# Delta * u of a unit in three transfers, and B and C laid out in DRAM in the order of the partitions

## The chip, the cores and the metric

The kernel runs on one core of one Trainium2 chip. The metric is the time of one execution on the device, in microseconds (us), less being better. The profile is one such execution; the median is taken over several. The engines are named as in the profile: PE (matrix engine; PEld is its weight load), DVE (vector engine), ACT (scalar engine), POOL (GpSimd) and SP (the sync engine, which only issues DMAs here). "SPq" is SP's queue of instructions.

## The reference

The reference is a network of four layers on an input of 4 images of 64 x 64 pixels with 96 channels. Layers 0 and 1 are the ones that matter here. Each normalises its input, projects it to E = 192 channels, applies a depthwise 3 x 3 convolution and SiLU, and then runs a selective scan in four directions (K = 4: rows, columns, and both reversed) along the L = 4096 pixels, with N = 16 states for each channel:

```
delta = softplus(dt_w @ dts + bias)          # [B, K, E, L]
dA = exp(delta[..., None] * A)               # A: [K, E, N]
h  = dA * h + delta[..., None] * b[:, :, None, :] * u[..., None]
y  = einsum('bken,bkn->bke', h, c)
```

`u` is the convolved input in the order of the direction; `b` and `c` (16 states each) and `dts` are projections of it that differ from pixel to pixel. The four directions' `y` are put back into the order of the pixels and added, a layer norm, a gate and an output projection follow, and the result is added to the input. Layers 2 and 3 are attention without softmax and a quantised MLP; the change doesn't touch them.

## The kernel before

**Phases.** `run` goes through four phases: two layers, each on two pairs of images. A phase has two stages. `prepare` convolves both images and computes, for every direction and every chunk of TC = 512 pixels, Delta (softplus), Delta * u, B and C, and stores them in DRAM; the `finish` of the phase before runs interleaved with it. `scan_phase` then does the recurrence. After the four phases `token_layers` does layers 2 and 3.

**What is in DRAM.** For each of the NC = 8 chunks there is `ph.delta[c]` (three bf16 parts of Delta), `ph.du[c]` with shape [2, G, E + PITCH, TC] in f32 (two equal copies of Delta * u; G = 8 is directions x images) and `ph.bc[c]` with shape [G, 2 * NS, TC] (B and C, 32 rows for each of the eight g). `steps` writes them: `bc` by a DMA on ACT's queue (line 301), the two copies of `du` by one DMA each on ACT's and SP's queue (line 319), Delta on ACT's queue (line 323).

**Units of the scan.** A scan's 128 partitions are 4 quarters x 8 g x 4 states; so partition 32 a + 4 g + s holds state 4 a + s of g. A unit is one chunk of 512 pixels and EB = 12 channels. A chunk has 16 units, a phase 128, and the four phases 512. For a unit the kernel

- loads Delta (`load_delta`, line 376, tile `dlt`, three buffers) and Delta * u (`load`, `load_quarters`, line 396) into `u.h`, [128, 12, 512] in f32, of which there are four buffers. The DMA reads each row of Delta * u four times, once for every state of a quarter. Each of the three groups of quarters (1 and 2 together, 0, 3) is loaded in two halves of 6 channels, so there are six transfers: two of 64 partitions and four of 32;
- multiplies `h` by B on POOL (`times_b`, line 406), three channels at a time, four instructions a unit;
- replicates Delta over the partitions on PE (line 412), takes exp(A * Delta) on ACT (line 416) and scans on DVE (line 423), one instruction for each of the 12 channels;
- contracts over the states with C on PE (line 441), evicts on ACT (line 453) and stores with four DMAs on SP's queue (`store`, line 461).

B and C are loaded once for a chunk (`load_b`, `load_c`; `load_states`, line 344) by four DMAs each, one for every quarter:

```
for a in range(4):
    self.nc.sync.dma_start(t[32 * a : 32 * a + 32], of[:, 4 * a : 4 * a + 4])
```

**The order.** `scan_phase` writes the order out by hand; no scheduler changes it. POOL's product runs half a unit (B_LEAD = 6 channels) ahead of the scan. At the last channel of a unit SP's queue gets, in this order, the four stores of the unit before, perhaps a load of B (after unit 8 of a chunk) or of C (after unit 15, two chunks ahead), then Delta and Delta * u of the unit three ahead. There are 7 loads of B and 6 of C inside each phase; one of B and two of C stand at its start.

**Semaphores of the DMAs.** The DMAs of all queues are dealt eight semaphores in turn; a DMA that gets one waits until the DMA that had it before, eight places earlier, has landed. Inside the scan all DMAs are SP's.

Of the kernel before, what the change touches and what calls it, by code (L numbers as in the profile page):

```python
# [9 lines left out]
F32 = mybir.dt.float32  # L10
# [14 lines left out]
NS = 16  # L25
R = 6
K = 4
G = 2 * K
PAD = HW + 2
TC = 512  # L30
NC = L // TC
ROWS = TC // HW
EB = 12
# [40 lines left out]
def rows(t):  # L74

    if len(t.shape) == 2:
        return t.rearrange("p (r w) -> p r w", w=HW)
    return t.rearrange("p h (r w) -> p h r w", w=HW)
# [49 lines left out]
class Scans:  # L128
# [19 lines left out]
    def prepare(self, ph):  # L148

        nc, cst, a, pre = self.nc, self.cst, self.a, ph.pre  # L150
        ph.gs = self.keep.tile([C, 2, 2], F32, name="gs", bufs=3)
        ph.delta = [
            self.dram.tile([NP16, G, E, TC], BF16, name="delta", bufs=2 * NC) for _ in range(NC)
        ]


        ph.du = [
            self.dram.tile([2, G, E + PITCH, TC], F32, name="du", bufs=2 * NC) for _ in range(NC)
        ]
        ph.bc = [self.dram.tile([G, 2 * NS, TC], F32, name="bc", bufs=2 * NC) for _ in range(NC)]  # L160
        ph.ud = self.dram.tile([C, 2, HW, 2, 64], F32, name="ud")
        ph.y = self.dram.tile([64, G, 2, 2, NEB, 16 * EB], F32, name="y")
        x = ph.x_in[ph.pair]

        with self.tc.tile_pool(name="prep", bufs=1) as wp, self.tc.tile_pool(
            name="steps", bufs=2
        ) as sp:

            def load(name, shape, at=0):
                t = wp.tile([at + shape[0]] + shape[1:], F32, name=name)  # L170
                nc.sync.dma_start(t[at:], a[pre + name])
                return t

            xp = load("x_proj", [C, 2, 2, XD2])
            dt_w = load("dt_w", [XD2 - 2 * NS, 2, E], at=2 * NS)
            conv_b = load("conv_b", [C, 2])
            ds = load("Ds", [C, 2, K])
            dsum = wp.tile([C, 2], F32, name="dsum")
            nc.vector.tensor_reduce(dsum, ds, mybir.AxisListType.X, ALU.add)
            yield  # L180


            st = wp.tile([C, 2, 8, 6], F32, name="st")
            with self.tc.tile_pool(name="stats", bufs=2) as rp:
                for hl in range(8):
                    raw = rp.tile([C, 8, 2, 64], F32, name="raw")
                    nc.sync.dma_start(raw, x[:, hl * 8 : hl * 8 + 8])
                    for i in range(2):
                        nc.vector.bn_stats(st[:, i, hl], raw[:, :, i])
                    yield  # L190
            for i in range(2):
                mv = wp.tile([C, 2], F32, name="mv")
                nc.vector.bn_aggr(mv, st[:, i].rearrange("p c s -> p (c s)"))
                ps = self.bank()
                nc.tensor.matmul(ps[:C, :1], cst.group, mv[:, 0:1], start=True, stop=True)
                gs = ph.gs[:, i]
                nc.vector.tensor_copy(gs[:, 0:1], ps[:C, :1])
                d = wp.tile([C, 1], F32, name="d")
                nc.vector.tensor_tensor(d, mv[:, 0:1], gs[:, 0:1], ALU.subtract)
                nc.vector.scalar_tensor_tensor(d, d, d, mv[:, 1:2], ALU.mult, ALU.add)  # L200
                ps = self.bank()
                nc.tensor.matmul(ps[:C, :1], cst.group, d, start=True, stop=True)
                ln = wp.tile([C, 2], F32, name="ln")
                neg_rsqrt(nc, cst, ps[:C, :1], ln[:, 0:1], gs[:, 1:2], ln[:, 1:2])
                nc.vector.tensor_scalar_mul(gs[:, 1:2], gs[:, 1:2], -1.0)
                yield
            in_w = wp.tile([C, E], F32, name="in_w")
            nc.sync.dma_start(in_w, a[pre + "in_proj_w"][:, :E])
            taps = wp.tile([C, 9, E], F32, name="taps")
            nc.sync.dma_start(taps, a[pre + "conv_w"].unsqueeze(0).broadcast_to([C, 9, E]))  # L210

            nc.vector.tensor_tensor(
                taps, taps, in_w.unsqueeze(1).broadcast_to([C, 9, E]), ALU.mult
            )

            xc = [wp.tile([C, 2, L], F32, name="xc", bufs=2) for _ in range(2)]
            yield from self.convolve(ph, 0, x, xc[0], taps, conv_b, dsum)
            ph.beside = 0.5
            other = self.convolve(ph, 1, x, xc[1], taps, conv_b, dsum)
            for i in range(2):  # L220
                for c in range(NC):
                    for k in range(2):
                        yield from self.steps(ph, sp, xc[i], xp, dt_w, i, k, c)
                        for _ in range(2):
                            next(other, None)
                            yield
                for _ in other:
                    yield
                ph.beside = 1.7
# [52 lines left out]
    def steps(self, ph, sp, xc, xp, dt_w, i, k, c):  # L282


        nc, cst = self.nc, self.cst
        u = scan_view(xc, k, c)
        ps = self.bank()
        for h in range(2):
            nc.tensor.matmul(rows(ps[:XD2]), xp[:, k, h], u[:, h], start=h == 0, stop=h == 1)  # L289
        xd = sp.tile([XD2, TC], F32, name="xd")  # L290

        nc.scalar.activation(xd[:XD], ps[:XD], AF.Identity, bias=cst.one_row[:XD])  # L292
        nc.scalar.activation(
            xd[64:], view(ps[64:XD2], TC - 1, (-1, TC)), AF.Identity, bias=cst.one_row[64:]
        )
        yield
        both = []
        for back in range(2):
            at = 64 * back
            g, cc = 2 * (k + 2 * back) + i, NC - 1 - c if back else c  # L300
            nc.scalar.dma_start(ph.bc[cc][g], xd[at : at + 2 * NS])
            both.append((g, cc, scan_view(xc, k + 2 * back, cc), self.p_d.tile([C, 2, TC], F32, name="d")))
        for m in range(2):
            for back, (_, _, _, ps) in enumerate(both):
                part = slice(64 * back + 2 * NS, 64 * back + XD)
                nc.tensor.matmul(  # L306
                    ps[:, m], dt_w[part, k, m * C : (m + 1) * C], xd[part], start=True, stop=True
                )
        yield
        for g, cc, u, ps in both:  # L310
            delta = sp.tile([C, 2, TC], F32, name="dl")
            parts = sp.tile([C, NP16, 2, TC], BF16, name="parts")
            du = sp.tile([C, 2, TC], F32, name="du_sb")
            nc.scalar.activation(delta, ps, AF.Softplus)  # L314
            nc.scalar.copy(parts[:, 0], delta)
            nc.vector.tensor_tensor(rows(du), rows(delta), u, ALU.mult)  # L316
            nc.vector.tensor_tensor(delta, delta, parts[:, 0], ALU.subtract)  # L317
            for copy, queue in enumerate((nc.scalar, nc.sync)):
                queue.dma_start(ph.du[cc][copy, g, :E].rearrange("(h e) t -> e h t", h=2), du)
            nc.gpsimd.tensor_copy(parts[:, 1], delta)  # L320
            nc.vector.tensor_tensor(parts[:, 2], delta, parts[:, 1], ALU.subtract)  # L321
            for h in range(2):
                nc.scalar.dma_start(
                    ph.delta[cc][:, g, h * C : (h + 1) * C].rearrange("n q t -> q n t"),
                    parts[:, :, h],
                )
            yield
# [10 lines left out]
        ph.carry = self.keep.tile([128, E], F32, name="carry")  # L338
        ph.b, ph.c, ph.cw = {}, {}, {}

    def load_states(self, t, of):

        for a in range(4):
            self.nc.sync.dma_start(t[32 * a : 32 * a + 32], of[:, 4 * a : 4 * a + 4])

    def load_b(self, ph, c):
        ph.b[c] = self.units.tile([128, TC], F32, name="b")
        self.load_states(ph.b[c], ph.bc[c][:, :NS])

    def load_c(self, ph, c):  # L350
        ph.c[c] = self.units.tile([128, TC], F32, name="c")
        self.load_states(ph.c[c], ph.bc[c][:, NS:])

    def weights(self, ph, c, op):

# [25 lines left out]
    def load(self, u):  # L381

        nc, ph = self.nc, u.ph
        u.h = self.units.tile([128, EB, TC], F32, name="h", bufs=4)
        self.load_delta(u)
        n = EB // 2
        for first, quarters in ((1, 2), (0, 1), (3, 1)):
            for e in range(0, EB, n):
                self.load_quarters(u, e, n, first, quarters)

    def load_quarters(self, u, e, n, first, quarters):

# [591 lines left out]
```

## Time and profile before

| | |
|---|---|
| median of 3 runs | 12483.71 us (12462.94 to 12492.15) |
| the profiled execution | 12443.48 us, its span 12441.7 us |
| mean granted PE clock | 0.665 |
| busy share of the span: PE, DVE, ACT, POOL | 81%, 75%, 58%, 59% |
| DMA | 2491.45 MB, 882704 packets, mean 200 GB/s |
| issues of h<-du | 1024 of 768.0 KB and 2048 of 384.0 KB |
| issues of b<-bc and of c<-bc | 128 each, of 64.0 KB |
| scans of the four phases, first to last | 1909.5, 1910.9, 1912.1 and 1928.4 us |

The span is cut by the profile into engines' busy shares, but the stages have different limits: the four scan phases take 7661 us of the 12442 together, and what a change inside them is worth is read from them. A DMA that the profile shows on SPq is only its issue; the data moves later, and the DMA share and GB/s tell of that. The DMA share is the mean over 16 DMA engines. In the chain of waits, "DMA h<-du" is the time in which the chain stood on a transfer of Delta * u.

### The profile page before, as it was taken

How to read it: one execution, taken by the hardware profiler on the slowest of the kernel's cores; microseconds unless marked ns; L12 is line 12 of the kernel's file. 1: busy time of each engine (PE TensorE's matmuls, PEld its weight loads, DVE VectorE, ACT ScalarE, POOL GpSimd, SP SyncE). 2: the span in 40 equal slices, each digit the busy share in tenths (PEclk: the TensorE clock that was granted, in tenths of full speed). 3: DMA queues.
4: the chain of work that ended last, by engine and by line, in shares of the span. 5: the costliest groups of instructions: out<-in, count | busy, mean ns of one | idle time of the engine just before them, and what ended most of it. 6: DMA issues, size and time to landing. Idle time of an engine off the chain costs nothing.

```text
span 12441.7 us, 340858 instructions
## 1 busy us (share of the span) xinstructions
PE 10107.0 (81%) x147008; PEld 4972.1 (40%) x147008; DVE 9376.9 (75%) x9235; ACT 7185.6 (58%) x11815; POOL 7386.0 (59%) x2316
## 2 busy tenths in 40 slices
PE   7758888879878888879878888888878888887777
PEld 2224444433334444433334444443334444444333
DVE  2479999963569999982469999992459999993567
ACT  2456666644456666653456666663446666662556
POOL 0159999950149998960139899880129989990000
PEclk8665565669675555659775656558776655557787
DMA  3567676754667676764566777664567666663110
GB/s 92 172 227 247 244 248 247 248 168 140 213 205 246 245 247 244 250 200 128 176 215 244 246 247 249 243 226 125 174 202 249 244 243 245 245 244 122 30 21 11
DMA packets 882704, 2491.45 MB, mean 200 GB/s; under 512 B 279058, under 2 KB 561840, under 8 KB 737456
## 3 DMA queue, kind: packets, MB, share of 16 engines
q1 hardware_dynamic: 552496, 2163.38, 50.6%
q10 hardware_dynamic: 328704, 306.26, 8.5%
q8 instruction: 1158, 18.97, 0.7%
q14 instruction: 346, 2.83, 0.1%
HBM read 1955.42 MB, written 513.80 MB: 198 GB/s over the span
## 4 chain that ended last, share of the span: by engine, by line
DMA 53%; PE 20%; SPq 8%; DVE 7%; ACT 4%; issue 4%; POOL 3%; ACTq 1%; POOLq 0%; DVEq 0%
DMA h<-du 47%; PE c L260 8%; SPq L396 7%; POOL h L406 3%; PE f L591 2%; DVE h L423 2%; PE d L306 2%; DMA yk<-y 1%; PE c L289 1%; PE f L600 1%; POOL parts L320 1%; PE f L682 1%; DMA du<-du_sb 1%; PE y L441 1%; DVE parts L321 1%
## 5 line engine op out<-in xcount | busy, mean ns | idle before, releaser
L406 POOL TENSOR_TENSOR h<-h,b 128x1536 f32<-128x1536 f32 x2048 | 7016.6, 3456 | 780.6 <-DMA h<-du 369.0
L423 DVE TENSOR_TENSOR_SCAN h<-a,carry,h 128x512 f32<-128x512 f32 x5376 | 6356.7, 1259 | 391.8 <-POOL h L406 360.9
L416 ACT ACTIVATE a<-a,a_col 128x512 f32<-128x512 f32 x6144 | 4030.3, 662 | 1966.6 <-PE a L412 1814.4
L441 PEld LDWEIGHTS y<-h,cw 128*32 128x32 f32 x131072 | 2886.3, 145 | 3597.6 <-issue 1606.1
L441 PE MATMUL y<-h,cw 128*32 128x48 f32 x131072 | 3702.1, 269 | 438.0 <-ACT a L416 216.9
L412 PE MATMUL a<-dlt,rep 24*128 24x512 bf16 x6144 | 3319.4, 551 | 884.8 <-DVE h L423 782.1
L320 POOL CAST parts<-dl 96x1024 bf16<-96x1024 f32 x256 | 341.3, 1348 | 3092.1 <-DVE dl L317 2785.6
L316 DVE TENSOR_TENSOR du_sb<-dl,xc 96x1024 f32<-96x1024 f32 x256 | 397.3, 1577 | 1296.2 <-ACT dl L314 1234.8
L453 ACT COPY d<-y 128x384 f32<-128x384 f32 x2048 | 979.6, 478 | 485.7 <-PE y L441 432.7
L260 PE MATMUL c<-xn,taps 96*96 96x512 f32 x2304 | 1034.1, 609 | 73.5 <-DVE xn L245 71.0
L423 DVE TENSOR_TENSOR_SCAN h<-a,h 128x512 f32<-128x512 f32 x768 | 869.6, 1201 | 189.0 <-ACT a L416 110.6
L412 PEld LDWEIGHTS <-rep 24*128 24x128 bf16 x6144 | 471.9, 101 | 903.6 <-issue 451.0
L306 PE MATMUL d<-xd,dt_w 7*96 7x512 f32 x1024 | 520.8, 859 | 254.9 <-ACT xd L292 225.6
L260 PEld LDWEIGHTS c<-xn,taps 96*96 96x96 f32 x2304 | 382.6, 167 | 707.5 <-issue 628.7
L823 POOL MEMSET tn<- 1x4096 f32 x8 | 27.8, 3506 | 865.0 <-PE pa L843 514.7
L267 ACT ACTIVATE xc<-c,conv_b 96x512 f32<-96x512 f32 x128 | 87.3, 682 | 718.1 <-PE c L260 633.2
L591 PE MATMUL f<-yk,perm 128*128 128x384 f32 x1024 | 415.9, 546 | 99.6 <-DMA yk<-y 88.8
L314 ACT ACTIVATE dl<-d 96x1024 f32<-96x1024 f32 x256 | 252.0, 1017 | 400.9 <-DMA delta<-parts 234.5
L321 DVE TENSOR_TENSOR parts<-dl,parts 96x1024 bf16<-96x1024 f32 x256 | 366.9, 1455 | 153.2 <-POOL parts L320 153.1
L289 PE MATMUL c<-xc,x_proj 96*103 96x512 f32 x512 | 420.2, 958 | 4.2 <-ACT xc L267 4.2
L306 PEld LDWEIGHTS d<-xd,dt_w 7*96 7x96 f32 x1024 | 151.7, 212 | 542.4 <-ACT xd L292 295.8
L360 ACT ACTIVATE cw<-c,gmask 128x256 f32<-128x256 f32 x512 | 287.9, 573 | 126.2 <-DMA h<-du 65.9
(114 smaller groups left out, 5650.6 us busy)
## 6 DMA issues: line engine op xcount, KB each, us to landing
h<-du SPq DMA_DIRECT2D x1024, 768.0 KB
h<-du SPq DMA_DIRECT2D x2048, 384.0 KB
delta<-parts ACTq DMA_DIRECT2D x512, 288.0 KB
dlt<-delta SPq DMA_DIRECT2D x512, 288.0 KB
du<-du_sb SPq DMA_DIRECT2D x256, 384.0 KB
du<-du_sb ACTq DMA_DIRECT2D x256, 384.0 KB
y<-d SPq DMA_DIRECT2D x2048, 48.0 KB
yk<-y SPq DMA_DIRECT2D x256, 384.0 KB
```

What stands on the lines that cost most here:

```text
L260: nc.tensor.matmul(rows(ps[:C]), taps[:, tap, h * C : (h + 1) * C], xn[:, ROWS * c + dy : ROWS * (c + 1) + dy, dx : dx + HW], start=tap == ...
L289: nc.tensor.matmul(rows(ps[:XD2]), xp[:, k, h], u[:, h], start=h == 0, stop=h == 1)
L306: nc.tensor.matmul(ps[:, m], dt_w[part, k, m * C : (m + 1) * C], xd[part], start=True, stop=True)
L321: nc.vector.tensor_tensor(parts[:, 2], delta, parts[:, 1], ALU.subtract)
L396: self.nc.sync.dma_start(u.h[32 * first : 32 * (first + quarters), e : e + n].rearrange("p e t -> p (e t)"), source.rearrange("a g e t -> ...
L406: self.nc.gpsimd.tensor_tensor(h, h, b, ALU.mult)
L412: self.nc.tensor.matmul(u.a[n], rep, u.dl[:, n], start=True, stop=True)
L416: self.nc.scalar.activation(u.a[n], u.a[n], AF.Exp, scale=u.ph.a_col[:, at : at + 1])
L423: self.nc.vector.tensor_tensor_scan(u.h[:, n], u.a.pop(n), u.h[:, n], 0.0 if u.c == 0 else u.ph.carry[:, at : at + 1], ALU.mult, ALU.add,)
L441: self.nc.tensor.matmul(view(u.y[32 * j : 32 * j + 32], l2 * EB, (8 * EB, 4), (1, EB)), u.ph.cw[u.c][:, l1, 8 * j + l2], view(u.h, 64 * l1 ...
L453: self.nc.scalar.copy(u.d[:, :, :, l1], u.y[:, : 32 * EB].rearrange("p (t h x) -> p t h x", t=4, h=2))
L591: nc.tensor.matmul(ps[:, : 4 * C].rearrange("p (w v e) -> p w v e", w=4, v=nv), cst.perm[:, k], view(t, off, (sw if k < 2 else -sw, 4), (1 ...
```

## The change

Three things are changed. Delta * u of a unit is loaded by one transfer for each of the three groups of quarters, with all 12 channels in it: three transfers, one of 64 partitions and two of 32, with rows of 12 x 512 f32 (24 KB) where they were 12 KB. In DRAM `ph.bc[c]` is laid out as [8, G, 4, TC]: first four blocks of 4 states of B, then four of C, and inside each block the eight g; this is the order of the scan's partitions. So B, or C, of a chunk is one contiguous piece of 128 rows, and `load_states` reads it by one DMA in place of four. The DMA of `steps` that stores B and C of one g writes 8 blocks of 4 rows, where it wrote 32 rows in a row. The number of stores, the order of the instructions on the other engines, and the buffers stay as they are.

```diff
-        ph.bc = [self.dram.tile([G, 2 * NS, TC], F32, name="bc", bufs=2 * NC) for _ in range(NC)]
+        ph.bc = [self.dram.tile([NS // 2, G, 4, TC], F32, name="bc", bufs=2 * NC) for _ in range(NC)]
...
-            nc.scalar.dma_start(ph.bc[cc][g], xd[at : at + 2 * NS])
+            nc.scalar.dma_start(ph.bc[cc][:, g], xd[at : at + 2 * NS])
...
-    def load_states(self, t, of):
+    def load_states(self, ph, c, first, name):
 
-        for a in range(4):
-            self.nc.sync.dma_start(t[32 * a : 32 * a + 32], of[:, 4 * a : 4 * a + 4])
+        t = self.units.tile([128, TC], F32, name=name)
+        of = ph.bc[c][first : first + NS // 4]
+        self.nc.sync.dma_start(t, of.rearrange("a g s t -> (a g s) t"))
+        return t
 
     def load_b(self, ph, c):
-        ph.b[c] = self.units.tile([128, TC], F32, name="b")
-        self.load_states(ph.b[c], ph.bc[c][:, :NS])
+        ph.b[c] = self.load_states(ph, c, 0, "b")
 
     def load_c(self, ph, c):
-        ph.c[c] = self.units.tile([128, TC], F32, name="c")
-        self.load_states(ph.c[c], ph.bc[c][:, NS:])
+        ph.c[c] = self.load_states(ph, c, NS // 4, "c")
...
-        n = EB // 2
         for first, quarters in ((1, 2), (0, 1), (3, 1)):
-            for e in range(0, EB, n):
-                self.load_quarters(u, e, n, first, quarters)
+            self.load_quarters(u, 0, EB, first, quarters)
```

In the built program each unit then has eight DMAs on SP's queue (four stores, Delta, three of h) where it had eleven.

## The prediction

> **What bounds the kernel now.** I first read the chain of waits on the page, then the costliest groups, then the timeline of the SP queue and of POOL in one stretch of the first scan phase, and last the windows over the same stretch.
>
> The chain says that the end is set in the four scan phases, by one transfer:
>
> ```profile
> DMA 53%; PE 20%; SPq 8%; DVE 7%; ACT 4%; issue 4%; POOL 3%; ACTq 1%; POOLq 0%; DVEq 0%
> DMA h<-du 47%; PE c L260 8%; SPq L396 7%; POOL h L406 3%; PE f L591 2%; DVE h L423 2%; PE d L306 2%; DMA yk<-y 1%; PE c L289 1%; PE f L600 1%; POOL parts L320 1%; PE f L682 1%; DMA du<-du_sb 1%; PE y L441 1%; DVE parts L321 1%
> ```
>
> The groups give the floors of the two busiest engines:
>
> ```profile
> L406 POOL TENSOR_TENSOR h<-h,b 128x1536 f32<-128x1536 f32 x2048 | 7016.6, 3456 | 780.6 <-DMA h<-du 369.0
> L423 DVE TENSOR_TENSOR_SCAN h<-a,carry,h 128x512 f32<-128x512 f32 x5376 | 6356.7, 1259 | 391.8 <-POOL h L406 360.9
> ...
> L423 DVE TENSOR_TENSOR_SCAN h<-a,h 128x512 f32<-128x512 f32 x768 | 869.6, 1201 | 189.0 <-ACT a L416 110.6
> ```
>
> There are 4 x 128 = 512 units. POOL needs 7016.6/512 = 13.7 us for one, DVE (6356.7 + 869.6)/512 = 14.1 us. From the scans' start times, the units of a whole chunk (16) take 241.6 us on average (chunks 1 to 6), 15.1 each: an ordinary unit 14.1 to 15, and two in each chunk 17 to 19. So something above DVE sets the pace. The windows (columns: stretch, its length, busy time of PE, PEld, DVE, ACT, POOL, PE clock, DMA share, GB/s) show what:
>
> ```profile
> 1469.00:1473.50 4.50, 3.55 (x87) 1.83 (x81) 3.59 (x5) 3.15 (x6) 4.50 (x2) 0.50 0.91 289
> 1474.50:1482.00 7.50, 6.80 (x135) 3.28 (x134) 7.50 (x8) 5.78 (x11) 7.50 (x3) 0.50 0.56 229
> ...
> 1496.00:1501.00 5.00, 3.92 (x70) 1.69 (x71) 4.78 (x5) 3.76 (x6) 3.94 (x2) 0.50 0.29 98
> 1503.00:1507.00 4.00, 3.94 (x80) 1.83 (x73) 4.00 (x4) 2.96 (x7) 4.00 (x2) 0.50 0.97 345
> ```
>
> The DMA share swings between nearly 1 (16 engines at work, the 64-partition transfers of h) and about half (the 32-partition ones run on 8 engines). I take it from the packet records (start, duration, size) that 8 engines are never idle in an ordinary unit: the median of the time with fewer than 8 packets in flight is 0.0 us a unit. **The eight DMA engines that every transfer uses are the bound**, just above DVE. The third row is the exception, 98 GB/s. The SP queue shows what happens there:
>
> ```profile
> 1488.47 4.19 SPq L461 DMA_DIRECT2D y<-d  x4
> 1493.93 6.19 SPq L344 DMA_DIRECT2D c<-bc  x4
> 1500.23 0.65 SPq L376 DMA_DIRECT2D dlt<-delta  x1
> 1501.06 4.06 SPq L396 DMA_DIRECT2D h<-du  x6
> ```
>
> Every DMA waits for the one eight places before it: eight semaphores are dealt out in turn. A load of h has six transfers, so the four of C wait for its third to sixth: the last C is issued (1499.48) only when the whole load has landed, and Delta and h of the next unit stand behind it. The engines run dry, and POOL pays one load later (last bracket: idle before, releaser):
>
> ```profile
> 1497.86 13.71 POOL L406 TENSOR_TENSOR h<-h,b 128x1536 f32<-128x1536 f32 x4 [1.06 <-DMA c<-bc]
> 1516.06 13.66 POOL L406 TENSOR_TENSOR h<-h,b 128x1536 f32<-128x1536 f32 x4 [4.48 <-DMA h<-du]
> ```
>
> From the packet records a chunk loses 5.7 us of eight-engine time on average (chunks 1 to 6 of all phases), nearly all of it in the units after its two loads, B and C: 2.85 us for each. Without that, and without the B and C packets (1.34 us a load, below), a unit costs these engines (241.6 - 5.7 - 2.7)/16 = 14.6 us.
>
> [...] In the trace, too, one of the eight landings of a transfer often comes 1 to 2 us after the other seven. [...]
>
> **The change part by part.**
>
> (a) *One transfer for B or C.* With 3 transfers of h a unit issues 4 stores of y, 1 Delta, 3 h: eight, as many as the semaphores, so each waits for its namesake of the unit before. The B or C shifts this by one: it waits for the last Delta, Delta for the first h, the first h for the second, the second h for the third. Estimate of the room: POOL starts on a unit when its h has landed, the scan follows 3.5 us later, so the previous unit's stores can be issued about 14.6 - 3.5 = 11.1 us before that landing; four stores (0.6 each) and Delta (0.7) later the first h is reached some 7.8 us ahead, or at worst when the second h lands, 3.7 us ahead (786 KB at 213 GB/s, which the records show with eight packets in flight). The engines never run dry. There are 7 such B and 6 such C loads a phase: 52 x 2.85 = **148 us** gained. Bounds 0 (a wait remains) and 166 (by DVE's excess, 3.2 us each).
>
> (b) *Engines for B and C.* Now 4 x 32 packets of 2 KB on 8 engines, 16 each; [...] At 84 ns (records) 0.67 us less, x52 = **35 us**. Bounds 0 and 50.
>
> (c) *24 KB rows.* A unit's h packets on a busy engine fall from 24 of 12 KB to 12 of 24 KB. Fastest packets: 2 KB 84 ns, 12 KB 460, 16 KB 611, so about 37 ns per KB and some 10 ns fixed. 12 x 10 ns = 0.12 us a unit, for some 125 units of 4 phases **60 us**. No packet of this path above 12 KB is there before, so both bounds are open: 32 ns fixed (slope 8 to 12 KB) would give 190, but DVE's floor caps it; and 24 KB packets may be slower, below.
>
> (d) *Halves given up.* POOL's first piece of a unit needed only the first halves, so five of the six transfers; now it needs all three. That is one 393 KB transfer, 1.85 us at 213 GB/s. The loop that could bind is: unit u ends, stores and issue 3.3 us, h 14.6, landing 1, POOL 3.5, scans 14.1, unit u+3 ends: about 37.1 us, now 38.9, against 3 x 14.5 = 43.5. It has 4.6 us to spare, so the delay is paid once a phase: **-7 us**. Bounds 0 and, if it shows after every dry spell, 100.
>
> (e) *SP.* Three issues less in each unit and three for each B or C, of about 0.65 us. Nothing: the queue waits for landings. If DMA were faster, these would be its margin.
>
> (f) *Stores of B and C* (256, ACT queue) now write 8 blocks of 4 rows, so 8 engines instead of 16: 4 packets each instead of 2, 0.17 us, x256 = 44 us of engine time in the preparation, where the DMA share is 0.35 to 0.57 and the chain names PE, DVE and POOL. Nothing; bounds 0 and 44 lost.
>
> Sum: 148 + 35 + 60 - 7 = 236 us. Against the profiled execution, 12443.5 us: 12207. The median of the runs shown is 40 us above it; on that, 12248, rounded to 12250.
>
> After it a unit costs DMA about 14.5 us, DVE 14.1: DMA still binds, and what is late next is POOL's wait for h.
>
> **Rivals.**
> *The dry spell stays* (10%): SP reaches the first h later than worked out, and the single B or C still empties the engines. Only b, c and d: 88 us, 12396. For it: SP is always late today. Against: it is late because of six transfers' semaphores.
> *DVE becomes the bound* (9%): a 24 KB packet saves 40 ns or more. A chunk then takes 16 x 14.1 = 225.6 us, 16 less, for 7 chunks of 4 phases 448 us: 12036. Against: the sizes' slope shows 10 to 32 ns.
> *24 KB packets are slow* (slower; 9%). Place: the eight busy engines, 12 packets a unit. Without c the gain is 176 us over 500 units, 0.35 us each, 29 ns a packet: from 3% over two 12 KB packets the gain is gone. At 8%, 74 ns, 0.88 us a unit, it is 12484 - 176 + 444 = 12752; at 5%, 46 ns, 12584. For it: instruction fetches of 16 KB take 945 ns or more in the records, far above the slope. Against: 16 KB rows of the output take 611 ns, on the slope.
> *Both cancel* (6%): 3%, about 12484.
>
> **How the numbers follow.** The sum as worked out has 66%, its own range 12160 to 12330 from the bounds of a to d. A measurement of this kernel can tell about 0.2%, 25 us, from no change. Faster 66 + 10 + 9 = 85%, same 6%, slower 9%. The range takes in the main case, the first rival and part of the second: 12080 to 12440.
>
> **What would show it.** Right: in the windows no stretch near 100 GB/s beside c<-bc or b<-bc; no unit of 17 us and more; POOL's wait for h<-du well under 369 us; h<-du still first in the chain; 24 KB packets at about 910 ns. Wrong: ordinary units above 14.6 us, packets above 950 ns, or dry spells still there.

## The result, and the profile after

The changed kernel is slower. Its median is 13285.36 us (13206.6 to 13376.66, 4 runs) against 12480.49 us (4 runs) for the kernel before: a ratio of 1.065, with a 95% interval of 1.058 to 1.072. The forecast was 12250, with a range that ended at 12440.

The profiled execution took 13300.82 us, its span 13299.0, which is 857 us more than before. All of it lies in the scan phases: first to last scan they take 2155.0, 2079.8, 2143.2 and 2148.3 us, 8526 together, against 7661. The preparation didn't change. Delta * u is now 512 issues of 1536 KB and 1024 of 768 KB. In what follows the three transfers of a unit are H1 (partitions 32 to 95), H2 (0 to 31) and H3 (96 to 127). By the records of the landings all 512 H1 ran on 16 engines and all 1024 H2 and H3 on 8. That it is the same eight each time is taken from the DMA share, which is only 0.48 between 1522 and 1525 us (windows below), with an H1, an H2 and an H3 under way at once. "The eight" are these engines.

The chain of waits of the kernel after, by engine and by line:

```profile
DMA 68%; PE 18%; DVE 4%; ACT 4%; issue 3%; SPq 1%; POOL 1%; ACTq 1%; DVEq 0%; POOLq 0%
DMA h<-du 63%; PE c L260 7%; PE f L589 2%; PE d L306 2%; DMA yk<-y 1%; PE c L289 1%; DMA delta<-parts 1%; PE f L598 1%; POOL parts L320 1%; PE f L680 1%; PE f L669 1%; DVE parts L321 1%; DVE dl L317 1%; DMA du<-du_sb 1%; PE f L655 1%
```

h<-du has grown from 47% to 63% of a longer span. SPq, which held 8% before, is down to 1%: the issuing of DMAs has left the chain, and their landing fills it. The costliest groups of POOL and DVE in the kernel after:

```profile
L404 POOL TENSOR_TENSOR h<-h,b 128x1536 f32<-128x1536 f32 x2048 | 7006.0, 3452 | 1638.9 <-DMA h<-du 857.8
L421 DVE TENSOR_TENSOR_SCAN h<-a,carry,h 128x512 f32<-128x512 f32 x5376 | 6364.2, 1259 | 1128.4 <-POOL h L404 1097.4
```

The work is the same to 0.2% (7006.0 and 6364.2 us of busy time). The idle time ahead of it is not: POOL's has doubled, DVE's has nearly trebled. The wait for h<-du, which was to fall well under 369 us, is 857.8.

The chain in one stretch of the first phase (start, length, what) shows the form of the new wait. Each piece runs from the issue of an H3 to its landing, and the next H3 is issued 0.02 us later:

```profile
1491.75 17.75 DMA h<-du
1509.50 0.02 issue
1509.52 17.86 DMA h<-du
1527.38 0.02 issue
1527.39 16.32 DMA h<-du
1543.72 0.02 issue
1543.74 16.82 DMA h<-du
```

An H3 is on its way for the whole of a unit. The timeline of SP's queue in the same stretch (a group of three starts with the issue of H1 and ends with that of H3):

```profile
1510.28 3.03 SPq L459 DMA_DIRECT2D y<-d  x4
1513.40 0.69 SPq L376 DMA_DIRECT2D dlt<-delta  x1
1516.10 11.96 SPq L394 DMA_DIRECT2D h<-du  x3
1528.16 3.27 SPq L459 DMA_DIRECT2D y<-d  x4
```

The stores and Delta are out early; the three transfers of h are not. In this group H1 is issued at 1516.10, H2 at 1521.54 and H3 at 1527.39 us, and by the records of the landings their namesakes of the unit before land at 1516.01, 1521.52 and 1527.38. So each of the three stands at the head of the queue until its namesake has landed, and with it all that is behind. In 444 of the 512 units the namesake is the DMA eight places before; a load of B or C, or the start of a phase, shifts the others. Over the whole kernel 93% of the H1, 97% of the H2 and 88% of the H3 are issued within 0.15 us of the landing of the DMA eight places before. The list of SP's waits for h, for the kernel after and then for the kernel before (us in total, times, longest):

```profile
SPq L394 <- DMA h<-du: 5192.1, 1395, 8.2
SPq L376 <- DMA h<-du: 117.8, 58, 4.0
```

```profile
SPq L396 <- DMA h<-du: 2039.9, 1326, 4.0
SPq L461 <- DMA h<-du: 633.0, 657, 2.8
SPq L376 <- DMA h<-du: 571.3, 450, 2.8
SPq L344 <- DMA h<-du: 277.5, 227, 2.9
```

That is 5310 us now against 3522 before. SP waited for h all along; it waits longer now.

The windows over the stretch (columns: stretch, its length, busy time of PE, PEld, DVE, ACT, POOL, PE clock, DMA share, GB/s) show what the engines of the DMA do meanwhile:

```profile
1519.00:1522.00 3.00, 2.81 (x67) 1.61 (x67) 3.00 (x4) 1.99 (x4) 3.00 (x2) 0.50 0.93 377
1522.00:1525.00 3.00, 2.80 (x55) 1.25 (x59) 3.00 (x4) 2.10 (x4) 1.34 (x1) 0.50 0.48 156
...
1527.40:1530.00 2.60, 2.28 (x65) 1.65 (x66) 0.00 (x0) 1.31 (x4) 2.46 (x1) 0.50 0.45 115
```

By the packet records 3.7 packets are in flight on average between 1527 and 1528 us, 2.2 in the next microsecond, 10 in the one after: seven of the eight have run out of work, one has not, and H3 lands only when that one is through. A unit of a chunk took 15.1 us on average before and takes 268.2/16 = 16.8 now.

The records of the landings tell how late that one is. Of the eight landings of a 32-partition transfer the last came 0.73 us after the seventh before the change (median) and comes **8.9 us** after it now. This distance is called the lag below. The spread, from the first of the eight landings to the last, was 2.9 us and is 10.2 us.

### The profile page after: what moved, and what is told of

Same layout as the page of the kernel before. It is cut to its first block, busy times and chain, and to the rows that moved or that the text cites. A ratio compares the mean times of both kernels' runs of the same rounds, so it can differ in the third digit from the quotient of the medians.

```text
span 13299.0 us, 337534 instructions
## 1 busy us (share of the span) xinstructions
PE 10412.3 (78%) x147008; PEld 5039.4 (38%) x147008; DVE 9386.3 (71%) x9235; ACT 7256.6 (55%) x11815; POOL 7377.9 (55%) x2316
## 4 chain that ended last, share of the span: by engine, by line
DMA 68%; PE 18%; DVE 4%; ACT 4%; issue 3%; SPq 1%; POOL 1%; ACTq 1%; DVEq 0%; POOLq 0%
DMA h<-du 63%; PE c L260 7%; PE f L589 2%; PE d L306 2%; DMA yk<-y 1%; PE c L289 1%; DMA delta<-parts 1%; PE f L598 1%; POOL parts L320 1%; PE f L680 1%; PE f L669 1%; DVE parts L321 1%; DVE dl L317 1%; DMA du<-du_sb 1%; PE f L655 1%
## 5 line engine op out<-in xcount | busy, mean ns | idle before, releaser
L404 POOL TENSOR_TENSOR h<-h,b 128x1536 f32<-128x1536 f32 x2048 | 7006.0, 3452 | 1638.9 <-DMA h<-du 857.8
L421 DVE TENSOR_TENSOR_SCAN h<-a,carry,h 128x512 f32<-128x512 f32 x5376 | 6364.2, 1259 | 1128.4 <-POOL h L404 1097.4
L410 PE MATMUL a<-dlt,rep 24*128 24x512 bf16 x6144 | 3589.2, 589 | 1423.2 <-DVE h L421 1342.8
L439 PEld LDWEIGHTS y<-h,cw 128*32 128x32 f32 x131072 | 2926.5, 149 | 3881.0 <-issue 1918.1
L410 PEld LDWEIGHTS <-rep 24*128 24x128 bf16 x6144 | 498.6, 103 | 1402.7 <-issue 890.4
```

Of the source, the lines that this page charges most:

```text
L404: self.nc.gpsimd.tensor_tensor(h, h, b, ALU.mult)
L410: self.nc.tensor.matmul(u.a[n], rep, u.dl[:, n], start=True, stop=True)
L421: self.nc.vector.tensor_tensor_scan(u.h[:, n], u.a.pop(n), u.h[:, n], 0.0 if u.c == 0 else u.ph.carry[:, at : at + 1], ALU.mult, ALU.add,)
L439: self.nc.tensor.matmul(view(u.y[32 * j : 32 * j + 32], l2 * EB, (8 * EB, 4), (1, EB)), u.ph.cw[u.c][:, l1, 8 * j + l2], view(u.h, 64 * l1 ...
```

## The experiments

All ratios are to the kernel before, measured with runs of it on the same chip, with 95% intervals.

**Which part costs: e1 and e2.** e1 is the kernel after with h in six transfers again, e2 the kernel before with h in three.

```diff
 e1, on the kernel after
+        n = EB // 2
         for first, quarters in ((1, 2), (0, 1), (3, 1)):
-            self.load_quarters(u, 0, EB, first, quarters)
+            for e in range(0, EB, n):
+                self.load_quarters(u, e, n, first, quarters)
 e2, on the kernel before: the same lines the other way round
```

> The changed kernel with Delta * u in six transfers again; only B and C are changed. Theory 1 (three transfers of h are dealt the eight semaphores so that each waits for its namesake of the unit before on the slowest DMA engine) and theory 2 (rows of 24 KB are slow where many engines are at work) both expect what the prediction had for B and C alone: no dry spell beside their loads, about 12484 - 183 = 12300 us. Theory 3 (the one transfer of B or C, or the 8-block stores, is what costs) expects 13200 us.

> The kernel before with Delta * u in three transfers; B and C as before. Theories 1 and 2: the whole loss, 13280 us or somewhat more, since B and C bring nothing. Theory 3: about 12420 us, as the prediction had for 24 KB rows.

e1 took 12415.0 us (0.9955, 0.9939 to 0.997), e2 13651.37 us (1.094, 1.091 to 1.097). So the three transfers of h are the cost, and B and C by one transfer are a gain, 59 us where the forecast for e1 had 183. e2 is slower than the 13280 us or somewhat more that were expected. In e1 the two units of 17.5 us in each chunk are gone, as forecast, but the other fourteen grew from 14.75 to 15.0 us. The parts don't add: with h in three transfers, loading B and C by one DMA each is worth 366 us (13651 to 13285), alone 59.

**The tie to the namesake: e3 and e8.** The 7979 DMAs of the kernel before carry eight semaphores, 997 or 998 DMAs each, and the 6251 of the kernel after the same eight, 781 or 782 each. In both traces no DMA is issued before the last one with its semaphore has landed; the soonest is issued 0.016 us after that. After the change a unit has eight DMAs, so each transfer of h waits for its namesake of the unit before. e3 adds one small DMA to each unit, on which nothing depends; then H1 waits for H2 of the unit before, H2 for its H3, and H3 for the small one. e8 adds a second: H1 waits for H3 of the unit before and Delta for its H2.

```diff
 e3, in load, behind the three transfers of h
+        spare = self.units.tile([G, 4], F32, name="spare")
+        nc.sync.dma_start(spare, self.a["gmask"][:G, :4])
 e8, behind that
+        spare = self.units.tile([G, 4], F32, name="spare_b")
+        nc.sync.dma_start(spare, self.a["gmask"][:G, 4:])
```

> The changed kernel with a ninth DMA in each unit, 8 rows of 16 bytes into a tile that nothing reads, behind the three of h: with nine, the first h waits for the second h of the unit before, the second for the third, the third for the small one. Theory 1: the namesakes are parted, as with eleven DMAs before, and the time comes back to 12250 to 12600 us; the late landing of one engine shrinks from about 11 us to a few. Theory 2: nothing is changed in the rows, 13200 to 13350 us.

> The kernel after with two small DMAs more a unit (a spare tile of G x 4, as in e3), so ten a unit on eight semaphores: the unit's first transfer of h waits for the third of the unit before, the Delta load for the second. If the tie to the namesake is what costs (theory 1), the tie is gone here too, but the Delta load and the first h come free only when the last transfers of the unit before have landed, so short dry spells of 1 to 2 us may come back: 12300 to 12700 us. If the size of the rows or of the transfers costs: 13200 us, as after.

e3 took 12335.02 us (0.9885, 0.986 to 0.991): 7% less than the kernel after, with the same packets and the same bytes, and one DMA more. e8 took 12344.46 us (0.9878, 0.9864 to 0.9893). The lag of the last engine fell from 8.9 us to 0.98 and 0.27. The chain of e3 in the same stretch, and POOL's group over the whole of e3:

```profile
1504.44 14.12 DMA h<-du
1518.56 0.02 issue
1518.57 0.68 SPq L396
1519.25 0.04 issue
1519.29 13.96 DMA h<-du
```

```profile
L406 POOL TENSOR_TENSOR h<-h,b 128x1536 f32<-128x1536 f32 x2048 | 7019.2, 3458 | 659.2 <-DMA h<-du 259.3
```

The pieces are 14 us in place of 17, and POOL's wait for h<-du is 259 us in place of 858. Both times lie in the ranges that theory 1 gave. Both versions beat the kernel before and the kernel after. With this order of the transfers, then, the number of DMAs in a unit is what made the change slow; e5 below has another order.

It isn't simply one wait more. In e3, too, a transfer of h is always on its way and another waits for it: here it is the landing of H3 that lets H2 of the next unit go. What is shorter is the time to that landing. Nine and ten DMAs make a transfer wait for a later one than its namesake, so SP runs ahead by less than a unit, and the engines of a transfer stay together (spread 3.3 and 0.7 us, against 10.2). Eight give it a lead of a whole unit, by which one engine can fall behind before anything stops the others. Whether it matters that the two are namesakes, or only that the lead is so long, no run tells apart.

**The rows: e4.** The kernel before with its six transfers cut by partitions, so that each has rows of 24 KB.

```diff
-            for e in range(0, EB, n):
-                self.load_quarters(u, e, n, first, quarters)
+            for z in range(2):
+                self.load_quarters(u, z, first, quarters)
...
+        at, p = u.eb * EB, 16 * quarters
...
-            u.h[32 * first : 32 * (first + quarters), e : e + n].rearrange("p e t -> p (e t)"),
+            u.h[32 * first + z * p : 32 * first + (z + 1) * p].rearrange("p e t -> p (e t)"),
...
-            .broadcast_to([quarters * G, NS // 4, n * TC]),
+            .broadcast_to([quarters * G, NS // 8, EB * TC]),
```

> The kernel before, six transfers of h on as many engines and of as many bytes as there, in the same order and with the same waits, but each with rows of 24 KB to half of the partitions in place of rows of 12 KB to all of them. Rows reach other partitions of their group than they should, so the values differ; the work is the same. Theory 1: as before or a little faster by the fewer packets, 12400 to 12500 us. Theory 2: most of the loss, 13000 us or more.

It took 16185.57 us (1.299, 1.294 to 1.304). Theory 2 had 13000 us or more, but this is over four times the loss of the change. This cut changed two things at once: the rows, and the number of partitions that a transfer's engines write (by the landings 16 engines write 32, or 8 write 16, where they wrote 64 and 32). Its 24 KB packets have a median of 1709 ns against 921 in the kernel after. It doesn't show that the rows are slow, since e3 has them and is fast; e12 below bears on the other reading.

**The order: e5, e6, e7, e13, e15.** The two smaller transfers of h swapped: in the kernel after (e5), the one before (e6), e1 (e7), e3 (e13) and e8 (e15).

```diff
-        for first, quarters in ((1, 2), (0, 1), (3, 1)):
+        for first, quarters in ((1, 2), (3, 1), (0, 1)):
```

> The changed kernel with the two 32-partition transfers of h swapped: quarters 1 and 2, then 3, then 0. Theory 4 ([...] the change lets the first h start while the third of the unit before is on the engines) expects that most of the loss goes: now it is quarter 0 beside which the first h starts. A unit then costs 13 us of the eight engines and DVE's 14.1 or a little more binds: 12050 to 12300 us. Theory 1 (each transfer waits for its namesake, one engine falls behind by most of a unit and paces the rest) has nothing changed by the order: 13150 to 13350 us.

> The kernel before with the same swap, six transfers and B and C as they were. Theory 4: the packets of the 64-partition transfers, which overlap with the last two of the unit before, come down from their 0.6 to 0.9 us toward 0.46; dry spells at B and C stay: 12150 to 12350 us. Theory 1: no change, 12440 to 12500 us.

> B and C as changed, Delta * u in six transfers, and the swap. Theory 4: 12050 to 12250 us, the dry spells gone too. Theory 1: as with B and C alone, 12400 to 12430 us.

> The kernel of e3 (nine DMAs a unit) with the two smaller transfers of h swapped: quarter 3 second, quarter 0 last. [...] quarter 0 in that place frees them, the 24 KB packets fall from a mean of 1075 ns towards 1018 (those of e8) and the kernel takes 12150 to 12280 us. If the swap is as harmful as it was for the kernel before (+1.9%), 12450 to 12600 us. If it makes no difference, 12335 us, give or take 30.

> The kernel of e8 (ten DMAs a unit) with the two smaller transfers of h swapped, quarter 3 before quarter 0. Here the large transfer of a unit waits for the last one of the unit before. If the swap costs something only because the large transfer runs beside one of the smaller ones (it added 1.3 to 2.7% to e3, e1 and the kernel before), nothing changes: 12344 us, give or take 30. If the order costs something by itself, 12480 to 12650 us.

| | time, us | ratio to before (interval) | the same without the swap |
|---|---|---|---|
| e5, on after | 12516.3 | 1.0013 (0.9996 to 1.0029) | 1.0649 |
| e6, on before | 12725.3 | 1.0187 (1.017 to 1.0204) | 1 |
| e7, on e1 | 12812.78 | 1.0257 (1.0238 to 1.0277) | 0.9955 |
| e13, on e3 | 12667.19 | 1.0133 (1.0116 to 1.015) | 0.9885 |
| e15, on e8 | 12602.09 | 1.0086 (1.0071 to 1.0101) | 0.9878 |

Without the tie the swap costs 1.9 to 3.0% (the text of e15 put its ends at 1.3 and 2.7; 1.3 is the ratio to before). With the tie it gains 6%. No forecast for e5, e6 or e7 held. Theory 4 had all three faster than they came out. Theory 1 had no effect of the order, which e5 contradicts: eight DMAs and the tie are still there, and most of the loss is gone. So the tie alone isn't enough; it is the tie together with the order quarter 0, then quarter 3. The lag falls from 8.9 to 2.0 us in e5, but mostly because two engines are behind now instead of one: the spread is still 7.6 us. e13 refuted the idea that quarter 0 in last place frees the packets: their mean stayed (1071 ns, 1075 in e3), and the time came out above all three forecasts. e15 refuted that the price comes only from the large transfer running beside a smaller one. Where the price of the swap comes from is open.

**The copy in DRAM and the pitch of Delta: e9 and e10.** e9 is the kernel after with quarters 0 and 3 read from each other's copy; e10 is e3 with four more rows in Delta's tile in DRAM.

```diff
 e9
-        copies = slice(0, 2) if quarters == 2 else slice(first % 2, first % 2 + 1)
+        copies = slice(0, 2) if quarters == 2 else slice(1 - first % 2, 2 - first % 2)
 e10
-            self.dram.tile([NP16, G, E, TC], BF16, name="delta", bufs=2 * NC) for _ in range(NC)
+            self.dram.tile([NP16, G, E + 4, TC], BF16, name="delta", bufs=2 * NC) for _ in range(NC)
```

> The kernel after, with the two copies of Delta * u in DRAM read the other way for quarters 0 and 3: quarter 0 from copy 1, quarter 3 from copy 0, with the bytes and the places in SBUF unchanged. If the lagging engine is made by two transfers that read the same copy in DRAM at once (theory: source), the lag and the time change: about 12500 us. If it is made on the side of SBUF [...] or by the order in which engines become free, nothing changes: 13250 us, give or take 100.

> The kernel of e3 (a ninth small DMA a unit) with the rows of Delta in DRAM 16 bytes further apart, 196624 instead of 196608 or as near as the layout gives it, so that the rows of one Delta load don't lie at a round distance. If Delta's rows meet in one part of DRAM and slow the 16-engine phases, 12150 to 12280 us; if not, as e3: 12335 us, give or take 30.

e9 took 13230.07 us (1.0592, 1.0545 to 1.0638), as the kernel after, with a lag of 8.9 us: which copy is read doesn't matter. e10 took 12385.53 us (0.9907, 0.989 to 0.9924), 50 us more than e3 and not faster. (The padding is 4 rows of 1 KB, so the distance is 200704 bytes, not the figure in the text above.)

**The partitions: e11, e12, e14.** e11 changes the order of the 128 partitions to 2 copies x 8 g x 8 states, with B, C and the constants laid out to match, so that h is one transfer (only the lines of the transfer are shown):

```diff
-        for first, quarters in ((1, 2), (0, 1), (3, 1)):
-            self.load_quarters(u, 0, EB, first, quarters)
+        nc.sync.dma_start(
+            u.h.rearrange("p e t -> p (e t)"),
+            ph.du[u.c][:, :, at : at + EB]
+            .rearrange("a g e t -> (a g) (e t)")
+            .unsqueeze(1)
+            .broadcast_to([2 * G, NS // 2, EB * TC]),
+        )
```

> Another order of the 128 partitions, so that the unit's Delta * u is one transfer of 128 rows of 24 KB over all 16 engines instead of three, and B and C one transfer each: six DMAs a unit. If the tie between the eight engines of one transfer and their namesakes is the cost, 16 engines in one transfer leave nothing to alternate, the DMA side drops below VectorE's 14.1 us a unit, and the kernel takes 12000 to 12100 us. If the engines hold each other up in one large transfer as well [...], it is above 12335 us.

It took 13901.53 us (1.112, 1.110 to 1.115). A window of e11:

```profile
1500.00:1515.00 15.00, 11.61 (x255) 6.28 (x255) 11.80 (x11) 8.87 (x16) 11.08 (x4) 0.69 0.99 217
```

All 16 engines are busy, at 217 GB/s. In the kernel after, a share of 0.93 moved 377 GB/s (the window from 1519 us above). The 24 KB packets of e11 have a median of 1851 ns, twice 921. e12 on e3, and e14 on the kernel after, test whether it matters which partitions the large transfer writes, with 0 to 63 instead of 32 to 95:

```diff
-        for first, quarters in ((1, 2), (0, 1), (3, 1)):
+        for first, quarters in ((0, 2), (2, 1), (3, 1)):
```

> The kernel of e3 (nine DMAs a unit) with another cut of the 128 partitions: the transfer over two quarters takes partitions 0 to 63 in place of 32 to 95, the two others take 64 to 95 and 96 to 127. Bytes, packets, copies read and engines are as in e3. [...] the four packets of the large transfer take 1.85 us each in place of some 0.91 to 1.1, the unit grows by 3 to 3.7 us and the kernel takes 13600 to 14200 us. If the slow packets of e11 come from its size or its source, nothing changes: 12335 us, give or take 50.

> The kernel after (eight DMAs a unit, so each transfer of h is tied to its namesake) with the cut of e12: partitions 0 to 63, then 64 to 95, then 96 to 127. [...] If the tie holds one engine 9 us behind only because its last transfer and the next unit's large one meet [...], the lag of the last engine is under 2 us and the time is that of e12: 13600 to 13750 us. If the tie alone makes a laggard, whatever meets, the lag stays at 6 us or more and the time is above 14300 us.

e12 took 13668.3 us (1.094, 1.093 to 1.096), inside its forecast of 13600 to 14200 for the case that the partitions matter. The mean 24 KB packet rose from 1075 to 1379 ns and the unit from 14.8 to 17.5 us. That is 2.7 us, a little less than the 3 to 3.7 of the forecast. The packets of over 1.5 us rose from 10% to 39% of all; the median stayed at 921 ns. With bytes, packets and number of engines unchanged, only the partitions can have done that. By what means they do it isn't shown, nor whether the slow packets of e4 (1709 ns) and e11 (1851 ns) have the same cause.

e14 took 13623.25 us (1.091, 1.088 to 1.094), the time of e12, but the lag stayed at 6.2 us. So each forecast got one half right: a lag of over 6 us arises with this cut of the partitions too, but here, at 17.4 us a unit against 17.5 in e12, it costs nothing more.

**Where the time of a transfer goes.** The packets of one engine follow each other closely (between 1524 and 1527 us of the kernel after, a 24 KB packet starts within 4 ns of the end of one before it, in 14 of 14 pairs), so the engine that lands last can be followed from the three Delta packets of a unit to the end of its H3. This worked for 271 to 408 of some 500 units in each kernel; the others are left out.

| | DMAs a unit, order | unit, us | spread, us | twelve 24 KB packets of the last engine, us |
|---|---|---|---|---|
| after | 8 | 16.8 | 10.2 | 14.0 |
| e2 | 8, more with B or C | 17.5 | 7.0 | 14.3 |
| e9 | 8 | 16.5 | 10.0 | 13.9 |
| e5 | 8, swapped | 15.1 | 7.6 | 12.6 |
| e3 | 9 | 14.8 | 3.3 | 11.8 |
| e8 | 10 | 14.9 | 0.7 | 11.9 |

In the kernel after the last engine is never idle: where two such units follow each other, most often 0.55 us, the time of the stores, lie between the end of one H3 and the next Delta. With 14.0 us for h and 1.8 for Delta that fills a unit. Its H1 packets take 0.92 to 1.03 us in the mean; those of H2 and H3, which go while the other seven are at the next unit's transfers, 1.04 to 1.61. So what costs the time directly is not that SP waits, nor that seven engines then stand idle, but that the packets of the engine behind have become slow. Its twelve packets are 2.2 us longer than in e3, and the unit 2.0. In all six kernels the unit goes with this sum, while a spread of 7.6 us with faster packets (e5) costs little. Why the packets are slow isn't shown.

Of the four reads of one row of Delta * u, the first is the slow one: 1.45 us on average in the kernel after, 1.29 in e3 and 1.27 in e8, over all engines from 1300 to 2450 us; the second to fourth have medians of 0.91 to 0.92 in all three. An example: seven engines begin an H3 of the kernel after between 1528.82 and 1528.91 us, and their first packets take 1.69 to 1.94 us, while the eighth, which begins its H1 at 1528.81, needs 0.91.

## Why the prediction was wrong, point by point

**The bound** was right: the eight engines, with DVE just below. In e3 a unit takes 14.8 us, 0.7 above DVE's 14.1.

**Step (a) failed**, at the sentence "each waits for its namesake of the unit before". The prediction saw this tie, worked out the waits of the units with a load of B or C, where it is shifted by one, and concluded "The engines never run dry". It didn't work out the other fourteen units of a chunk. There the shift is missing, each transfer of h waits for its namesake, and the sum has no term for that. The prediction knew of an engine behind ("one of the eight landings of a transfer often comes 1 to 2 us after the other seven") but took a transfer's landing as 786 KB at 213 GB/s, 3.7 us, as if all eight ended together. In the kernel after the lag is 8.9 us. In the ordinary units seven of the engines do run dry (lost eight-engine time, counted as in the prediction, is 1.05 us a unit against 0.2 in e3), and the eighth, which never does, needs 14.0 us for its packets of h in place of 11.8. The units are 2.0 us longer than in e3 (16.8 against 14.8). A ninth DMA, on which nothing depends, takes the 950 us back. That the wait could be so dear only with this order of the transfers (e5), and why the packets go slow, the runs leave open.

The part of (a) that was about B and C came out in mechanism and not in size. In e1 the 17.5 us units are gone, which is 2 x 2.5 = 5 us a chunk against the 5.7 of the forecast; the lost eight-engine time of a chunk falls from 5.7 to 1.0 us. But the other units gave 14 x 0.25 = 3.5 us back, and (a) and (b) together brought 59 us in place of 183. The 0.67 us of (b) is borne out as far as the engines go: by the landings each of the 256 loads of B and C ran on 8 engines before, and each of the 64 runs on 16 after, with 8 of its 128 packets for each. The lag was up there too (0.73 to 1.35 us); what makes those 0.25 us isn't shown.

**Step (c)**: right in its size. The fastest 24 KB packets take 909 ns, against 2 x 458 for the two that they replace: 7 ns saved, 10 forecast. The rival "24 KB packets are slow" falls: the median is 921 ns, and e3 is fast with them. The mean of 1128 ns is above the mark of 950 that was to show the prediction wrong, but the mark was no good sign: packets of the same size have means of 1075 in e3 and 1018 in e8, which are fast, and two 12 KB packets of the kernel before took 2 x 550 = 1100. (The instruction fetches in the rival's favour take 876 ns at the fastest; nine in ten take the 945 that it names, or more.) Fewer and larger transfers weren't faster here: with three transfers of h in place of six (e2) the kernel took 1.094 times as long as before, with one (e11) 1.112 times.

**Step (d)** can't be seen apart. e3 is 80 us below e1, where (c) less (d) gave 53; but e3 has nine DMAs a unit and e1 eleven, so this is no clean measure. The loop in (d) adds up to 36.5 us, not 37.1, which changes nothing. **Step (e)** is right as far as it went: the chain has SPq at 1%. **Step (f)** is right: the phases grew by 865 us and the span by 857, so the preparation didn't get longer. By the landings the 256 stores of B and C ran on 16 engines before and on 8 after, as it had them.

**The rivals.** "The dry spell stays" came nearest in kind, but it looked for the spell at the loads of B and C; it came in the ordinary units, to seven of the eight engines, and it was not what cost the time. None of the rivals held a wait of a transfer for its own namesake. **What would show it** was well chosen for saying that it was wrong: ordinary units above 14.6 us, POOL's wait above 369 us. Beside the loads of b the windows even show 111 GB/s (at 1466 to 1472 us, DMA share 0.43).

## What to carry to other kernels

Count the DMAs of a loop's round against the semaphores that are dealt out, eight here. Where the two counts were equal, each transfer waited for itself, one round earlier, and one engine of a split transfer fell 8.9 us (median) behind the others in a round of 16.8; one small DMA more (e3) turned 6.5% slower into 1.2% faster. Merging transfers can bring a loop to that count. It isn't a rule that such a count is slow: with two transfers swapped the kernel took as long as before (e5). So try one DMA more, and the order too. Take a split transfer's landing as that of its last engine (0.73 us after the seventh before the change, 8.9 after it), and work out the ordinary round as carefully as the exceptional one.

## What was not expected of the hardware

- One engine of eight can stay 8.9 us (median) behind the others, while all of them have equal shares of h and Delta. It is never idle, and still doesn't catch up, because its packets are slow while the others are at work (1.04 to 1.61 us in the mean for H2 and H3, against 0.92 to 1.03 for H1). Why they are slow stays open: e9 rules out the copy that is read (the lag stays at 8.9 us), and e14 shows a lag of 6.2 us with another cut of the partitions.
- The partitions that a transfer writes changed the speed of packets: with the 64-partition transfer on 32 to 95, 10% of the 24 KB packets took over 1.5 us (e3); with it on 0 to 63, 39% did (e12).
- Of four packets that read the same row of DRAM one after the other, the first is the slow one (1.27 to 1.45 us on average, against medians of 0.91 to 0.92).
- The order of two 32-partition transfers is worth 1.9 to 3.0% where there is no tie (e6, e7, e13, e15), and 6% the other way where there is one (e5).
